# Convolution block by lookup: weight preparation set by the image's rhythm, sums in place, a product split 7 to 2, ranking without negation, an earlier norm and scatter

## The chip, the cores and the metric

One core of a Trainium2 chip runs the kernel. The metric is the device time of one execution in microseconds (us). Before the change three runs took 2664.11, 2668.53 and 2668.79 us; the median is 2668.53. The engines are named as in the profile: PE (TensorE matmuls), PEld (its weight loads), DVE (VectorE), ACT (ScalarE), POOL (GpSimd), SP (the queue that issues most DMAs).

## The reference

Sixteen images of 256 channels and 28 x 28 pixels. The convolutions are replaced by a soft lookup: each channel's 3 x 3 patch is compared with 16 centroids, a softmax of the negated distances gives 16 weights, and these weigh rows of a table.

```python
def amm_conv3x3(x, centroids, w_sub):
    p = patches of x, as (B, pixels, C, 9)
    d = sum(p*p) - 2 * einsum('bncs,cks->bnck', p, centroids) + sum(centroids*centroids)
    attn = softmax(-d, axis=-1)                       # over the 16 centroids
    lut = einsum('cks,cso->cko', centroids, w_sub)
    return einsum('bnck,cko->bno', attn, lut)

def block(h):                                         # h = group norm of x
    out = relu(bn1(amm_conv3x3(h, centroids1, wsub1)))
    out = bn2(amm_conv3x3(out, centroids2, wsub2))
    out = out * sigmoid(relu(mean(out) @ w1 + b1) @ w2 + b2)
    return relu(out + h)

x = x + block(group_norm(x))
```

## The kernel before

**Blocks and steps.** Two layers (`l` = 0, 1) of 16 images (`b`). An image has 256 channels in two halves (`hh`) and 28 rows in two halves (`t`), so four blocks. Work of all engines is put into one list, `at(step, sub, function, ...)`, and issued in the order of (step, sub); each engine, and each DMA queue (SP's and POOL's), then runs its own instructions strictly in that order. A block takes two steps, an image eight; image n of the 32 starts at step 8n. Below, the position of a step is its number modulo eight, and sub orders work inside a step.

**A block.** `patches` loads nine shifted copies of the map from a DRAM copy (`home1`, `home2`) into `pt`, two steps ahead (SP, sub 1.5). `logits` (L386) multiplies by centroids into PSUM (`lg`), ACT takes the exponential (L397). `num_b` (L450) and `num_a` (L436) turn the weights into eight channels' lookup sums and denominators; DVE forms the reciprocal (L478), spreads it (L493) and scales (L512), POOL scales one pair and the ninth tap (L501). Each block ends with nine operands `q` of 128 x 392: four pairs `mm` (taps k = 2mm and 2mm + 1) and a single one (tap 8).

**Products.** The four blocks of an image would need eight products with quarter matrices A11, A12, A21, A22. The kernel uses a Strassen-like form with seven products: sums of the matrices (S1 to S4) and differences of operands, `mix` on POOL (L527, L529). `PRODUCTS` says at which step, relative to 8n, each product runs (sub 2.0) and over which taps; the product of S1 is cut into two parts, at steps 6 and 7. KO is the order of taps, (2, ..., 8, 0, 1); the mixes run in the order of pairs 1, 2, 3, tap 8, pair 0. The five mixes that make S1's operand start at step 5, sub 2.5. Results are put together by `acc_copy`, `acc_add` (L551, L557, L559) and `reg_add` (L564) in `hpads` (one tile of 128 x 900 for each half of the channels); c11, c12, c21, c22 are the quarters (channel half, row half).

**End of an image in layer 0.** `norm_out` (L571, ACT) applies batch norm and ReLU to a quarter, in place. `to_home2` (L592, POOL) then scatters `hpads[o]` to `home2` in DRAM, sorted by a channel ranking, as an indirect DMA in two shifts r = 0 and 1; the four scatters of an image write one tensor, so each waits for the landing of the one before. The next image's `acc_copy` writes the same `hpads`. Image 0 is put aside first (`d_h0`) and scattered later (`h0_load`, `h0_put`), because the ranking comes from its own result: `code_load`, `code_spread` (L612 to L625, DVE, from the centroids of layer 2), `rank_score`, `rank_make` (L652, L653) and so on, in steps 8 to 20.

**Group norm** of the next image runs beside: `gn_stats` (position 0), `gn_mean` (position 1, sub 2.1), `gn_var` (position 3, sub 2.1), each with a small matmul (L324, L338) whose PSUM bank is also used by the `nb` that follows; `gn_apply` and `to_home1` at position 4.

**Preparing the weights of layer 2** during layer 0, because they must be sorted by the ranking: `codes_load` and `codes_put` (centroids), `sub_load` and `sub_put` (the table's weights, 1.15 MB for each half, scattered to `d_wa` and `d_wb`, L680), `prep_wd0` to `prep_wd4` (the centroid matrix: nine small DMAs L717, two products on DVE L726, squares on POOL L285, matmuls L290, sums), `prep_cw0`, `prep_cwa` (L757), `prep_cwb` (L765 to L767), `sums_load`, `sums_put` (S1 to S4 of layer 2, L794). All of them go through one staging buffer `st` of 128 x 1568 (`stage()`), so a new load waits until the last use of the one before is over, and what stands behind it on SP waits too. In layer 2 this buffer serves a numeric safeguard.

Of the kernel before, what the change touches and what calls it, by code (L numbers as in the profile page):

```python
# [17 lines left out]
P = 128  # L18
# [7 lines left out]
K = 16  # L26
# [17 lines left out]
    (5, "A11", 0, KO), (6, "S1", 0, KO[:8]), (7, "S1", 0, KO[8:]), (8, "S3", 1, KO), (9, "S2", 0, KO),  # L44
# [31 lines left out]
def kernel(  # L76
# [530 lines left out]
    def code_spread(o):  # L607
        c2 = idx.pop("c2")
        mean = small.tile([P, S], F32, name="cmean")
        g = c2[:, : S * K].rearrange("p (s k) -> p s k", k=K)  # L610
        d = c2[:, 256 : 256 + S * K].rearrange("p (s k) -> p s k", k=K)
        nc.vector.tensor_reduce(csum[:, o : o + 1], c2[:, : S * K], axis=AX.X, op=ALU.max)  # L612
        nc.vector.tensor_scalar_mul(c2[:, 512 : 512 + S * K], c2[:, : S * K], -1.0)
# [4 lines left out]
        nc.vector.tensor_scalar_mul(mean, mean, 1.0 / K)  # L618
        nc.vector.tensor_sub(d, g, mean.unsqueeze(2).to_broadcast([P, S, K]))
        nc.vector.tensor_scalar_max(c2[:, 256 : 256 + S * K], c2[:, 256 : 256 + S * K], 0.0)  # L620
# [84 lines left out]
    def sub_load(o, part):  # L705
        n = 4 * C if part < 2 else C
        nc.sync.dma_start(stage()[:, :n], wsub2[o * P : (o + 1) * P, part * 4 * C : part * 4 * C + n])

    def sub_put(o, part):
        n = 4 * C if part < 2 else C  # L710
        scatter(d_wa if part < 2 else d_wb, 2 + part, o, pw["st"][:, :n])

    def prep_wd0():
        st = stage()
        nc.gpsimd.memset(st[:, :512], 0.0)
# [21 lines left out]
    def prep_wd4():  # L737
        st = pw.pop("st")
# [3 lines left out]
        nc.sync.dma_start(d_wd[1], st[:, 512:1536])  # L742
# [17 lines left out]
    def prep_cwb(part):  # L760
# [7 lines left out]
        if part == 3:  # L768
            pw.pop("st")
            nc.sync.dma_start(d_cwb, st[:, 512:1536])  # L770

    def sums_load(k0):
        st = stage()
        n = min(2, NS - k0)
        for hh in range(2):
            for o in range(2):
                at0 = 256 * (2 * hh + o)
                if n == 2:
                    nc.sync.dma_start(
                        st[:, at0 : at0 + 256].rearrange("p (s n) -> p s n", n=P),  # L780
                        view(d_wa, (hh * 8 + k0) * P * C + o * P, [[C, P], [P * C, 2], [1, P]]),
                    )
                else:
                    nc.sync.dma_start(st[:, at0 : at0 + P], d_wb[hh * P : hh * P + P, o * P : (o + 1) * P])

    def sums_put(k0):
        st = pw.pop("st")
        n = min(2, NS - k0)
        f = {w: st[:, 256 * i : 256 * i + P * n] for i, w in enumerate(("A11", "A21", "A12", "A22", "S1"))}
        for dst, a, b, op in (  # L790
            ("S1", "A21", "A22", ALU.add), ("A21", "A11", "A21", ALU.subtract),
            ("A22", "S1", "A11", ALU.subtract), ("A12", "A12", "A22", ALU.subtract),
        ):
            nc.gpsimd.tensor_tensor(f[dst], f[a], f[b], op)  # L794
        for n0, w in (("S1", "S1"), ("S3", "A21"), ("S2", "A22"), ("S4", "A12")):
            nc.sync.dma_start(d_ws[n0][:, k0 : k0 + n, :], f[w].rearrange("p (s n) -> p s n", n=P))
# [156 lines left out]
    for l in range(2):  # L953
        for b in range(B):
# [30 lines left out]
            if l == 0:  # L985
                for o in range(2):
# [65 lines left out]
    at(49, 0.6, prep_wd0)  # L1052
    at(50, 0.3, prep_wd1)
    for part in range(3):
        at(51 + 2 * part, 0.02, prep_wd2, part)
        at(51 + 2 * part, 2.1, prep_wd3, part, 51 + 2 * part)
    at(59, 1.9, prep_wd4)
    at(60, 0.6, prep_cw0)
    at(61, 1.9, prep_cwa)
    for part in range(4):  # L1060
        at((67, 68, 75, 76)[part], 2.3, prep_cwb, part)
    at(92, 2.3, load_se)
    for n in range(5):
        at(82 + 8 * n, 0.6, sums_load, 2 * n)
        at(83 + 8 * n, 2.3, sums_put, 2 * n)
# [196 lines left out]
```

## Time and profile before

| what | value |
|---|---|
| median of three runs | 2668.53 us |
| profiled execution | 2669.58 us |
| its span, first to last instruction | 2668.1 us |
| granted clock of PE, mean | 0.994 |
| HBM read, written | 288.93 MB, 79.80 MB |
| `e<-lg` L397 on ACT, 960 times | 821 ns each |
| `qp<-qp,qp` L529 on POOL, 512 times | 1868 ns each |
| `home<-hpad,col` L592 on POOL, 60 times | 1006 ns each; POOL idle before them 180.7 us |

The profiled execution is a separate run, 1.05 us above the median. A line of the timeline reads: start, duration, engine, line of the kernel, operation, what is written and read, shape, count, and in brackets how long the engine stood idle before it and what ended that. PE is busy nearly all the time in every fortieth of the span but the first. PE's granted clock is below 1 only in short stretches: it was 0.50 over 53.8 to 60.6, 122.1 to 125.5, 255.2 to 262.0, 432.7 to 436.1 and at the very end.

PE's own waits between 40 us and the first `nb` of image 14 at 1192.95 us, the longest of them:

| PE waits before | for | us in total, times, longest |
|---|---|---|
| acc L520 | POOL qp L529 | 6.7, 13, 1.5 |
| lg L386 | DVE qp L512 | 6.7, 4, 2.6 |
| nb L450 | DVE gn_dv L330 | 3.7, 1, 3.7 |
| lg L386 | DVE half_sum L557 | 2.1, 1, 2.1 |
| sqp L290 | ACT e L397 | 0.9, 1, 0.9 |
| lg L386 | DMA pt<-home | 0.7, 1, 0.7 |

### The profile page before, as it was taken

The numbers are of one execution on the slowest core, as the hardware profiler recorded it, in microseconds if no ns is written. First come the engines' busy times: TensorE is split into PE (matmuls) and PEld (weight loads), VectorE is DVE, ScalarE is ACT, GpSimd is POOL, SyncE is SP. The second block draws the span as 40 slices with busy tenths as digits, with TensorE's granted clock in tenths as the row PEclk, the third lists the DMA queues.
The fourth block names the chain that finished last, engine by engine and source line by source line (L and its number), as shares of the span: only waits on it lengthen the run. The fifth ranks groups of instructions, "written<-read, shape, count | busy, mean of one in ns | idle before, by whom it ended". The sixth has DMA issues, their size and how long they took to land.

```text
span 2668.1 us, 85705 instructions
## 1 busy us (share of the span) xinstructions
PE 2602.3 (98%) x36984; PEld 1261.0 (47%) x36984; DVE 1773.3 (66%) x3784; ACT 1356.5 (51%) x1874; POOL 1901.2 (71%) x1334
## 2 busy tenths in 40 slices
PE   5899999999999999999999999999999999999997
PEld 2444444444444454444444444444444444444444
DVE  4785666667666656566567767667767667767675
ACT  3344444444444544444455555555555555555653
POOL 3755677656776666776577777788777788787786
PEclk9999999999999999999999999999999999999999
DMA  8556557655567666565574555454445454555451
GB/s 197 156 150 176 157 140 204 185 158 139 142 167 180 175 157 161 147 175 155 136 190 110 114 120 122 117 123 107 118 119 127 113 122 105 120 124 126 114 116 50
DMA packets 219241, 374.39 MB, mean 140 GB/s; under 512 B 30360, under 2 KB 189128, under 8 KB 218856
## 3 DMA queue, kind: packets, MB, share of 16 engines
q1 hardware_dynamic: 211912, 334.87, 51.3%
q0 software_dynamic: 6944, 33.95, 3.6%
q8 instruction: 295, 4.83, 0.8%
q14 instruction: 90, 0.74, 0.1%
HBM read 288.93 MB, written 79.80 MB: 138 GB/s over the span
## 4 chain that ended last, share of the span: by engine, by line
PE 83%; POOL 3%; DMA 3%; issue 1%; ACT 1%; DVE 1%; POOLq 0%; DVEq 0%; ACTq 0%
PE acc L520 44%; PE lg L386 15%; PE na L436 12%; PE nb L450 12%; DMA home<-hpad,col 3%; POOL qp L529 2%; POOL qo L527 0%; POOL home L592 0%; ACT e L397 0%; PE sep L816 0%; PE sep L805 0%; DVE qp L512 0%; DVE rb L493 0%; ACT hpad L571 0%; ACT qo L470 0%
## 5 line engine op out<-in xcount | busy, mean ns | idle before, releaser
L397 ACT ACTIVATE e<-lg 128x784 f32<-128x784 f32 x960 | 738.2, 821 | 704.2 <-PE lg L386 699.6
L529 POOL TENSOR_TENSOR qp<-qp,qp 128x784 f32<-128x784 f32 x512 | 944.2, 1868 | 166.1 <-DVE qp L512 165.6
L520 PE MATMUL acc<-qp,w_S 128*128 128x392 f32 x2048 | 743.3, 503 | 7.8 <-POOL qp L529 6.9
L493 DVE STREAM_SHUFFLE rb<-r 128x392 f32<-128x392 f32 x1024 | 550.2, 603 | 0.0
L520 PE MATMUL acc<-qp,w_A 128*128 128x392 f32 x1536 | 546.6, 499 | 0.0
L520 PEld LDWEIGHTS acc<-qp,w_S 128*128 128x128 f32 x2048 | 376.3, 191 | 356.6 <-POOL qp L529 38.3
L386 PE MATMUL lg<-pt,wd 32*32 32x392 f32 x16384 | 495.7, 505 | 25.8 <-DMA pt<-home 8.1
L520 PEld LDWEIGHTS acc<-qp,w_A 128*128 128x128 f32 x1536 | 284.5, 190 | 247.0 <-DVE qp L512 40.0
L512 DVE TENSOR_TENSOR qp<-na,rb 128x784 f32<-128x784 f32 x352 | 333.3, 971 | 91.6 <-PE na L436 80.7
L464 DVE SCALAR_TENSOR_TENSOR r<-nb,kst,r 128x392 f32<-128x392 f32 x128 | 79.9, 624 | 462.3 <-ACT r L460 448.7
L450 PE MATMUL nb<-e,cwb 64*32 64x392 f32 x8192 | 378.2, 499 | 4.5 <-DVE gn_dv L330 3.7
L436 PE MATMUL na<-e,cwa 64*32 64x392 f32 x8192 | 374.4, 492 | 0.9 <-ACT e L397 0.7
L478 DVE RECIPROCAL r<-r 128x392 f32<-128x392 f32 x128 | 333.2, 2603 | 4.4
L501 POOL TENSOR_TENSOR qp<-qp,rb 128x784 f32<-128x784 f32 x160 | 296.9, 1866 | 2.4
L501 POOL TENSOR_TENSOR qo<-qo,rb 128x392 f32<-128x392 f32 x128 | 131.3, 1026 | 200.1 <-DVE rb L489 200.0
L450 PEld LDWEIGHTS nb<-e,cwb 64*32 64x32 f32 x8192 | 181.5, 108 | 194.3 <-issue 50.9
L386 PEld LDWEIGHTS lg<-pt,wd 32*32 32x32 f32 x16384 | 126.7, 103 | 306.2 <-issue 251.3
L436 PEld LDWEIGHTS na<-e,cwa 64*32 64x32 f32 x8192 | 182.4, 106 | 183.9 <-issue 74.0
L592 POOL DMA_INDIRECT home<-hpad,col x60 | 60.4, 1006 | 180.7 <-DMA home<-hpad,col 78.6
L460 ACT ACTIVATE r<-nb,kst 128x392 f32<-128x392 f32 x128 | 86.7, 678 | 180.2 <-PE nb L450 180.1
L421 POOL TENSOR_TENSOR z<-z,mx 128x1568 f32<-128x1568 f32 x32 | 92.0, 2875 | 86.3 <-DVE mx L415 86.3
L506 ACT COPY qp<-na 128x784 f32<-128x784 f32 x160 | 130.0, 812 | 24.3 <-PE na L436 22.8
(153 smaller groups left out, 1742.7 us busy)
## 6 DMA issues: line engine op xcount, KB each, us to landing
pt<-home SPq DMA_DIRECT2D x768, 209.0 KB
pt<-home SPq DMA_DIRECT2D x756, 104.5 KB
home<-xpad SPq DMA_DIRECT2D x31, 899.0 KB
xt<-in_x SPq DMA_DIRECT2D x30, 784.0 KB
out_dram<-y SPq DMA_DIRECT2D x32, 392.0 KB
w_S<-d_wS SPq DMA_DIRECT2D x4, 576.0 KB
st<-in_wsub SPq DMA_DIRECT2D x4, 512.0 KB
st<-d_wa SPq DMA_DIRECT2D x16, 128.0 KB
```

Of the source, the lines that this page charges most:

```text
L386: nc.tensor.matmul(bk[32 * c : 32 * c + 32, :N].rearrange("p (r w) -> p r w", w=W), lhsT=wts["wd", u["hh"]][32 * i : 32 * i + 32, mm, c, : ...
L397: nc.scalar.activation(eg[:, 2 * i : 2 * i + 2, :], bk[:, :, :N], AF.Exp, scale=2.0)
L421: nc.gpsimd.tensor_tensor(zk, zk, mx.unsqueeze(2).to_broadcast([P, N // 4, K]), ALU.subtract)
L436: nc.tensor.matmul(bs[32 * i : 32 * i + 32, r, :N], lhsT=wts["cwa", u["hh"]][64 * r : 64 * r + 64, mm, i, :], rhs=es[64 * r : 64 * r + 64, ...
L450: nc.tensor.matmul(bs[32 * i : 32 * i + 32, r, :N], lhsT=wts["cwb", u["hh"]][64 * r : 64 * r + 64, mm, i, :], rhs=es[64 * r : 64 * r + 64, ...
L478: nc.vector.reciprocal(u["r"], u["r"])
L493: nc.vector.stream_shuffle(rb[:, r, :], u["r"], mask_of(2 * mm + r))
L501: nc.gpsimd.tensor_tensor(q, q, u.pop(("rb", mm)), ALU.mult)
L506: nc.scalar.copy(pair(u, mm), u.pop(("na", mm))[:, :, :N])
L512: nc.vector.tensor_mul(pair(u, mm), u.pop(("na", mm))[:, :, :N], rb)
L520: nc.tensor.matmul(accs[key][:, :N], lhsT=wl[w][:, k, :], rhs=us["q", k], start=first and n == 0, stop=last and n == len(ks) - 1,)
L529: nc.gpsimd.tensor_tensor(pair(out_u, mm), pair(in0, mm), pair(in1, mm), ALU.subtract)
```

## The change

Five things. The product of S1 is cut 7 to 2 instead of 8 to 1. `code_spread` no longer negates the codes to find the largest magnitude: it takes the minimum and combines it. In layer 0, `norm_out` of c11 moves from sub 1.9 to 0.95 of step 8n + 12, the first scatter of `hpads[0]` from 1.95 to 0.96 (the second stays, at 1.97). The weight sums are formed in place, three taps at a time (three rounds instead of five), with load, sums and store in three different steps. And all of the preparation gets new steps and subs: loads at sub 2.6, behind the patches of the step, and POOL's work mostly at odd positions; `sub_load` brings two parts for each half instead of three, and clearing and storing become functions of their own.

```diff
 PRODUCTS = (
-    (5, "A11", 0, KO), (6, "S1", 0, KO[:8]), (7, "S1", 0, KO[8:]), (8, "S3", 1, KO), (9, "S2", 0, KO),
+    (5, "A11", 0, KO), (6, "S1", 0, KO[:7]), (7, "S1", 0, KO[7:]), (8, "S3", 1, KO), (9, "S2", 0, KO),
...
         nc.vector.tensor_reduce(csum[:, o : o + 1], c2[:, : S * K], axis=AX.X, op=ALU.max)
-        nc.vector.tensor_scalar_mul(c2[:, 512 : 512 + S * K], c2[:, : S * K], -1.0)
         m2 = small.tile([P, 1], F32, name="cm2")
-        nc.vector.tensor_reduce(m2, c2[:, 512 : 512 + S * K], axis=AX.X, op=ALU.max)
-        nc.vector.tensor_scalar_max(csum[:, o : o + 1], csum[:, o : o + 1], m2[:, 0:1])
+        nc.vector.tensor_reduce(m2, c2[:, : S * K], axis=AX.X, op=ALU.min)
+        cs = csum[:, o : o + 1]
+        nc.vector.scalar_tensor_tensor(cs, m2, -1.0, cs, op0=ALU.mult, op1=ALU.max)
...
     def sub_load(o, part):
-        n = 4 * C if part < 2 else C
+        n = (4 + part) * C
         nc.sync.dma_start(stage()[:, :n], wsub2[o * P : (o + 1) * P, part * 4 * C : part * 4 * C + n])
     def sub_put(o, part):
-        n = 4 * C if part < 2 else C
-        scatter(d_wa if part < 2 else d_wb, 2 + part, o, pw["st"][:, :n])
+        scatter(d_wa, 2 + part, o, pw["st"][:, : 4 * C])
+        if part == 1:
+            scatter(d_wb, 4, o, pw["st"][:, 4 * C : 5 * C])
+    def prep_clear():
+        nc.gpsimd.memset(stage()[:, :512], 0.0)
...
+    def prep_keep(dst):
+        nc.sync.dma_start(dst, pw.pop("st")[:, 512:1536])
...
     def sums_load(k0):
-        n = min(2, NS - k0)
+        n = min(3, NS - 1 - k0)
+        for w, t in sums_of().items():
+            hh, o = {"A11": (0, 0), "A21": (0, 1), "A12": (1, 0), "A22": (1, 1)}[w]
+            nc.sync.dma_start(
+                t[:, : n * P].rearrange("p (s n) -> p s n", n=P),
+                view(d_wa, (hh * 8 + k0) * P * C + o * P, [[C, P], [P * C, n], [1, P]]),
+            )
+            if n < 3:
+                nc.sync.dma_start(t[:, n * P :], d_wb[hh * P : hh * P + P, o * P : (o + 1) * P])
+    def sums_make():
+        f = sums_of()
+            ("A22", "A21", "A22", ALU.add), ("A21", "A11", "A21", ALU.subtract),
+            ("A11", "A22", "A11", ALU.subtract), ("A12", "A12", "A11", ALU.subtract),
+            nc.gpsimd.tensor_tensor(f[dst], f[a], f[b], op)
+    def sums_put(k0):
+        for n0, w in (("S1", "A22"), ("S3", "A21"), ("S2", "A11"), ("S4", "A12")):
+            nc.sync.dma_start(d_ws[n0][:, k0 : k0 + 3, :], f[w].rearrange("p (s n) -> p s n", n=P))
...
-                at(g + 12, 1.9, norm_out, l, b, *c11)
+                at(g + 12, 1.9 if l else 0.95, norm_out, l, b, *c11)
...
-                            at(g + 12 + o + (o and r), (1.95, 1.96)[r] if o == 0 else (1.805, 2.9)[r], to_home2, b, o, r)
+                            at(g + 12 + o + (o and r), (0.96, 1.97)[r] if o == 0 else (1.805, 2.9)[r], to_home2, b, o, r)
...
-        at(20 + 3 * o, 0.6, h0_load, o)
+        at(24 + 2 * o, 0.6 + 2 * o, h0_load, o)
         for r in range(2):
-            at(*(((21, 1.77), (22, 2.95)), ((24, 2.95), (25, 1.78)))[o][r], h0_put, o, r)
-        at(32 + 2 * o, 0.6, codes_load, o)
+            at(25 + 2 * o + r, 0.2 if r else 1.9, h0_put, o, r)
+        at(32 + 2 * o, 2.6, codes_load, o)
         for i in range(2):
-            at(33 + 2 * o, 1.78 if o == i == 0 else 1.805, codes_put, o, i)
-        for part in range(3):
-            c = 36 + 6 * o + 2 * part
-            at(c, 0.6, sub_load, o, part)
-            at(c + 1, (1.77, 2.7, 1.78, 1.805)[(3 * o + part) % 4 if o == 0 else (3, 0, 1)[part]], sub_put, o, part)
-    at(49, 0.6, prep_wd0)
-    at(50, 0.3, prep_wd1)
+            at(33 + 2 * o, 1.9, codes_put, o, i)
+        for part in range(2):
+            c = 40 + 8 * o + 2 * part
+            at(c, 2.6, sub_load, o, part)
+            at(c + 1, 1.9, sub_put, o, part)
+    at(56, 1.95, prep_clear)
+    at(57, 1.6, prep_wd0)
+    at(60, 0.3, prep_wd1)
     for part in range(3):
-        at(51 + 2 * part, 0.02, prep_wd2, part)
-        at(51 + 2 * part, 2.1, prep_wd3, part, 51 + 2 * part)
-    at(59, 1.9, prep_wd4)
-    at(60, 0.6, prep_cw0)
-    at(61, 1.9, prep_cwa)
+        c = (65, 67, 73)[part]
+        at(c, 0.02, prep_wd2, part)
+        at(c, 2.1, prep_wd3, part, c)
+    at(75, 1.9, prep_wd4)
+    at(75, 2.7, prep_keep, d_wd[1])
+    at(80, 2.6, prep_cw0)
+    at(82, 1.9, prep_cwa)
     for part in range(4):
-        at((67, 68, 75, 76)[part], 2.3, prep_cwb, part)
+        at((83, 84, 91, 92)[part], (2.3, 1.5, 2.3, 1.5)[part], prep_cwb, part)
+    at(92, 2.7, prep_keep, d_cwb)
     at(92, 2.3, load_se)
-    for n in range(5):
-        at(82 + 8 * n, 0.6, sums_load, 2 * n)
-        at(83 + 8 * n, 2.3, sums_put, 2 * n)
+    for n in range(3):
+        at(96 + 8 * n, 2.6, sums_load, 3 * n)
+        at(97 + 8 * n, 1.9, sums_make)
+        at(98 + 8 * n, 2.6, sums_put, 3 * n)
```

More of the change, by code (lines that the diff above doesn't have):

```diff
@@ L705, in sub_load @@
     def sub_load(o, part):
-        n = 4 * C if part < 2 else C
+        n = (4 + part) * C
         nc.sync.dma_start(stage()[:, :n], wsub2[o * P : (o + 1) * P, part * 4 * C : part * 4 * C + n])
     def sub_put(o, part):
-        n = 4 * C if part < 2 else C
-        scatter(d_wa if part < 2 else d_wb, 2 + part, o, pw["st"][:, :n])
+        scatter(d_wa, 2 + part, o, pw["st"][:, : 4 * C])
[3 more added lines that the diff above has]
+        nc.gpsimd.memset(stage()[:, :512], 0.0)
     def prep_wd0():
-        st = stage()
-        nc.gpsimd.memset(st[:, :512], 0.0)
+        st = pw["st"]
         for s in range(S):
@@ L737, in prep_wd4 @@
     def prep_wd4():
-        st = pw.pop("st")
+        st = pw["st"]
         center_mean(st[:, 512:1536], 1024, nc.gpsimd)
@@ L741, in prep_wd4 @@
         nc.gpsimd.tensor_sub(f, f, kbias.unsqueeze(1).to_broadcast([P, 32, 32]))
-        nc.sync.dma_start(d_wd[1], st[:, 512:1536])
+    def prep_keep(dst):
+        nc.sync.dma_start(dst, pw.pop("st")[:, 512:1536])
     def prep_cw0():
@@ L767, in prep_cwb, with sums_of @@
             nc.gpsimd.tensor_add(f[:, m], f[:, m], ones_b[:, m % 4, :].unsqueeze(1).to_broadcast([P, 4, 32]))
-        if part == 3:
-            pw.pop("st")
-            nc.sync.dma_start(d_cwb, st[:, 512:1536])
+    def sums_of():
+        return {w: pw["st"][:, 3 * P * i : 3 * P * i + 3 * P] for i, w in enumerate(("A11", "A21", "A12", "A22"))}
     def sums_load(k0):
-        st = stage()
-        n = min(2, NS - k0)
[L775 to L789, printed above, removed]
+        stage()
+        n = min(3, NS - 1 - k0)
[7 more added lines that the diff above has]
+                nc.sync.dma_start(t[:, n * P :], d_wb[hh * P : hh * P + P, o * P : (o + 1) * P])
```

6 lines of the change are left out of this document (2 added, 4 removed).

## The prediction

> **What bounds the kernel now.** I read the page first, then the same stretch image by image, then timelines where an image is long.
>
> ```profile
> span 2668.1 us, 85705 instructions
> PE 2602.3 (98%) x36984; PEld 1261.0 (47%) x36984; DVE 1773.3 (66%) x3784; ACT 1356.5 (51%) x1874; POOL 1901.2 (71%) x1334
> PE 83%; POOL 3%; DMA 3%; issue 1%; ACT 1%; DVE 1%; POOLq 0%; DVEq 0%; ACTq 0%
> ```
>
> TensorE is the bound. The change takes no matmul away, so it can only win where TensorE stands still or is clocked down; the chain's shares of POOL and DMA (3% each) say that there is something. The next view cuts the trace at the first `nb` matmul (L450) of an image; columns are length, busy time of each engine, granted clock, DMA share, GB/s. The rows are images 1, 2, 4, 5, 6, 9, 13 and 14 of the first layer.
>
> ```profile
> 122.27:206.35 84.08, 81.83 (x1154) 39.12 (x1154) 62.88 (x144) 36.58 (x50) 50.80 (x38) 0.98 0.54 141
> 206.35:292.38 86.03, 84.05 (x1166) 41.39 (x1155) 51.70 (x124) 37.68 (x52) 58.48 (x58) 0.96 0.63 170
> 373.07:456.78 83.71, 81.63 (x1167) 39.47 (x1155) 51.08 (x120) 38.00 (x52) 56.73 (x43) 0.98 0.66 180
> 456.78:539.55 82.77, 81.00 (x1166) 39.00 (x1155) 50.99 (x120) 37.90 (x52) 55.21 (x42) 1.00 0.62 168
> 539.55:624.42 84.87, 82.74 (x1170) 39.93 (x1160) 55.14 (x125) 38.12 (x52) 54.41 (x41) 1.00 0.61 158
> 786.43:867.27 80.84, 80.40 (x1166) 39.15 (x1155) 50.99 (x120) 38.00 (x52) 56.16 (x50) 1.00 0.64 162
> 1111.01:1192.95 81.94, 81.16 (x1165) 39.16 (x1154) 50.97 (x120) 37.95 (x52) 54.73 (x42) 1.00 0.62 164
> 1192.95:1273.00 80.05, 80.05 (x1164) 38.77 (x1153) 48.73 (x111) 37.99 (x52) 53.59 (x43) 1.00 0.58 149
> ```
>
> Image 14 has PE busy for all of its 80.05 us, and so have the images after it (80.42 us in layer 2). I take it as the ruler. Images 1 to 13 together are 30 us longer than 13 times 80.05, and the stall of 3.7 us before image 1 comes on top: some 34 us is all there is to win. Laying each run of matmuls of an image beside the same run of image 14 shows where each lags; these lags are the terms below. (0.12 us that images 1 to 13 all show at their end is not counted. A position is a step modulo eight.)
>
> **A: ranking without negation.** Before image 1, `nb` waits 3.71 us for DVE's group-norm work, which is queued behind the code ranking:
>
> ```profile
> 113.51 6.33 DVE L613 TENSOR_SCALAR c<-c 128x144 f32<-128x144 f32 x1
> 120.67 0.17 DVE L618 TENSOR_SCALAR cmean<-cmean 128x9 f32<-128x9 f32 x1
> 121.22 0.23 DVE L620 TENSOR_SCALAR c<-c 128x144 f32<-128x144 f32 x1
> ```
>
> ```profile
> 114.32 2.65 POOL L211 TENSOR_TENSOR w_S<-w_A,w_S 128x1152 f32<-128x1152 f32 x1
> 117.87 1.87 POOL L501 TENSOR_TENSOR qp<-qp,rb 128x784 f32<-128x784 f32 x1
> ```
>
> The negation (L613) takes 0.22 us in the other half at 140.37, but 6.33 us here: it ends at 119.84, 0.1 us after POOL's unbroken run of 112.51 to 119.74. Taking it out removes the stall only if the instructions behind it do not stand in the same place: L618 (9 columns) and L620 (144) are of the same kind, and at 141.41 L618 took 0.91 us, until a POOL instruction ended. Most such waits in this trace end at the next POOL boundary (L653 twice 1.93 to 1.95 us, L726 1.03 and 2.07); this one missed three. If L618 and L620 get in at 116.96 and 117.94, DVE is at the group norm by about 119, the 3.7 us wait shrinks below 1 and the half clock that follows it (0.50 over 122.1 to 125.5, 1.58 us of lag) goes: 4.3 to 5.3 us. If they too wait to 119.74, only the removed L613 and its neighbour's order are saved, 0.5 us. I take 3.0, between both, nearer the end that most rows show. The new two-operand maximum replaces L616 (0.21 us) and costs the same.
>
> The Trainium skill, SBUF — State Buffer, section "Who interferes with whom", says that a Vector instruction with two SBUF inputs also contends with a GpSimd instruction that reads SBUF. The trace agrees in one place: beside DVE's sum L211 at 94.79 (1.42 us) a POOL L529 took 2.99 us, its mean being 1.87. By that rule the new maximum may stand where the negation stood; A would be 0.5.
>
> **B: norm and scatter a stage sooner, product split 7 to 2.** At the end of an image POOL scatters `hpads` in four pieces, each waiting for the one before to land:
>
> ```profile
> 734.09 1.09 POOL L592 DMA_INDIRECT home<-hpad,col  x1 [3.14 <-ACT hpad L571]
> 740.67 0.97 POOL L592 DMA_INDIRECT home<-hpad,col  x1 [5.49 <-DMA home<-hpad,col]
> 748.23 1.03 POOL L592 DMA_INDIRECT home<-hpad,col  x1 [1.24 <-PE acc L520]
> 749.29 5.49 POOL L529 TENSOR_TENSOR qp<-qp,qp 128x784 f32<-128x784 f32 x3
> 755.71 1.85 POOL L529 TENSOR_TENSOR qp<-qp,qp 128x784 f32<-128x784 f32 x1
> ```
>
> ```profile
> 757.61 0.93 PE L520 MATMUL acc<-qp,w_S 128*128 128x392 f32 x2 [0.39 <-POOL qp L529]
> ```
>
> The five differences for S1 start behind the third piece, the last of them (pair 0, taps 0 and 1) ends at 757.56, and S1's last tap of that step waits. In the worst image, 2, the second piece landed so late that ACT's copy into `hpads` stood, and all of ACT with it:
>
> ```profile
> 252.31 0.49 ACT L551 COPY hpad<-acc 128x392 f32<-128x392 f32 x1 [8.26 <-DMA home<-hpad,col]
> ```
>
> With the norm at 0.95, ACT can do it after the two exponentials that end at 728.86, as c11's sum is done on DVE about 1 us earlier: 0.72 us, so the first piece is issued near 730 instead of 734.1, the second near 736.5 instead of 740.7. The third is then bound by POOL's scaling, not by a landing; the differences start 1 to 3 us sooner. By the split, pair 0 is needed only in the next step, some 5 us later. One tap (0.66 us on PE) moves from one step to the next, so PE's sum is the same; in layer 2, where PE never idles, it costs nothing. Queued behind the earlier pieces on POOL is only the scaling of the next step, which waits for DVE anyway (1.6 us at 904.36). Lags that go: image 2 5.86, image 3 0.53, image 5 2.60, images 8 to 13 0.62, 0.67, 1.08, 1.00, 1.18, 1.38. Sum 14.9, at least 12 if image 2 keeps half.
>
> **C: preparation moved.** Image 4 loses 3.53: SP's load of weights stands until the scatter of 413.23 lands at 420.82, the patches behind it go out 1.4 us late, logits wait 2.08 and run at half clock after it (0.50 over 432.7 to 436.1). The new loads sit at 2.6, behind the patches. Image 6 loses 0.77 and 0.44 to nine patch-delaying DMAs (0.57 us each) of prep_wd0 and to its two DVE products, 3.0 us long against POOL; they move to 1.6 and to position 4, where POOL is nearly idle. Image 7's 1.06 and image 13's 0.39 are late transfers and side work. Sum 6.2, at least 3.
>
> What the new places cost: prep_cwa now stands in position 2 ahead of the scaled copies. In image 10 DVE is free there at 876.69, POOL busy until 877.87, and the first L512 starts at 879.12. Four products of 0.34 (the shortest L757) from 877.87 end at 879.2, then the sum and two shuffles of 1.6 us: L512 is 1.8 late, the second logits, at 880.83, have 0.75 slack after its end at 880.08, so 1.1 is lost; 0 to 3 by the long L757 of 1.96. The three squares' matmuls all fall on group-norm steps as one did before; that one cost 1.27, the others 0.65 and 1.50, so 0.1 more. The sums become 12 POOL instructions of about 0.84 (L285, same 384 columns) in 3.48 us of idle POOL before the image, and 12 stores for 20 and 16 loads for 20; one instruction too long at most delays differences with 4.9 us of slack. h0's second scatters wait on POOL for a landing (2.9 to 7.6 us by L680) ahead of differences with that slack; SP's waits at 2.6 stand where it would wait for logits. Unbooked collisions: I put 1.0, 0 to 9. Rank_make's 2.26 in image 1 stays.
>
> **Sum.** 3.0 + 14.9 + 6.2 - 1.1 - 0.1 - 1.0 = 21.9. The profiled execution took 2669.58 (span 2668.1 and 1.5 around it), 1.05 above the median of 2668.53. 2669.58 - 21.9 = 2647.7; on the scale of the median 2646.6. I say 2647.
>
> **Rivals.**
> 1. The port wait passes on: the new maximum, L618 or L620 ends at 119.8. For it: L613 itself, three missed boundaries. Against: all other rows. A is 0.5, 2.5 less: 2649.1. Chance 0.24. The two-input rule above leads here.
> 2. Collisions in the new places: three of the preparation scatters (steps 28, 43, 75) hold POOL just ahead of the first piece of `hpads`, and three images lose what images 4 or 5 lost (2.6 to 3.5): 9 more, 2656. For it: each scatter blocks 1 us and lands in up to 7.6. Against: the split. Chance 0.12.
> 3. Little changes: differences still start late, as DVE's shuffles, not the scatters, release POOL, and the moved stalls come back elsewhere one for one; A alone is left, 2666. Against: image 14 with its third piece at 1234.93 lost nothing. Chance 0.08.
> 4. Slower: the first piece now runs beside the patches of its step (issued 2 us after it), they land late, and logits wait as in image 4, 2.08 and 1.42 at half clock, in all 15 scattering images: 52 - 22 = 30 more, 2699. It decides once patches land after the step's first logits; so far they were late at 549.46 (0.70) and in image 4 after 1.4 us of delay. Against: before, the piece ran beside the same patches' tails and the stores to home1. Chance 0.06.
>
> **How the numbers follow.** My forecast has 0.50; its own range is 2643 to 2652. With rivals 1 and 2 it makes 0.86; 2641 (A at 5.3, nothing lost in the new places, 1 us of spread between runs) to 2658 holds 0.8 of it all. About 0.2% (5.3 us) is what a measurement of this kernel can tell from no change: faster 0.86, same 0.08, slower 0.06.
>
> **What would show it.** Right: images 2 to 13 at 80.1 to 81, only those with square matmuls (7 and 8) and cwa (10) above; no PE wait on POOL L529 at S1; first piece about 24 us after an image's first `nb` instead of 28.4; clock at 1.00 from 135 on; DVE's reduction behind L612 short and the 3.7 us wait under 1. Wrong: a DVE TENSOR_SCALAR ending at 119.8 (rival 1), POOL's L592 with long waits behind a preparation scatter (2), logits waiting for `pt` (4).

## The result, and the profile after

The changed kernel takes 2652.59 us (median of 4 runs, 2650.44 to 2653.86) where before took 2668.66 beside it (4 runs): the ratio is 0.9942, with a 95% interval of 0.9925 to 0.9959. It is faster, by 16.1 us; the forecast was 21.9 less. The profiled execution took 2652.68, against 2669.58 before, so the traces account for 16.9.

The page of the profile has the same three lines to compare:

```profile
span 2651.2 us, 85709 instructions
PE 2594.3 (98%) x36984; PEld 1265.2 (48%) x36984; DVE 1771.8 (67%) x3782; ACT 1356.7 (51%) x1874; POOL 1901.3 (72%) x1326
PE 96%; DVE 2%; DMA 1%; issue 0%; POOL 0%; SPq 0%; ACT 0%; another core or an unknown queue 0%; DVEq 0%; POOLq 0%
```

In the chain of waits (last line) TensorE went from 83% to 96%, POOL from 3% to 0%, DMA from 3% to 1%: POOL's part of the chain is gone. DVE, which was at 1%, is at 2%.

The same cut by image, at the first `nb` matmul; rows are images 2, 4, 8, 9 and 14 (length, busy time of PE, PEld, DVE, ACT, POOL, clock, DMA share, GB/s):

```profile
203.16:285.00 81.84, 81.79 (x1164) 39.86 (x1154) 51.78 (x124) 37.99 (x52) 56.67 (x55) 1.00 0.61 160
366.31:446.93 80.62, 80.58 (x1166) 39.98 (x1155) 50.95 (x120) 37.89 (x52) 54.72 (x41) 1.00 0.63 169
690.37:773.20 82.83, 82.06 (x1170) 40.06 (x1159) 52.09 (x122) 38.02 (x52) 53.07 (x40) 1.00 0.55 149
773.20:853.23 80.03, 80.03 (x1166) 39.38 (x1155) 54.71 (x122) 38.12 (x52) 56.24 (x40) 1.00 0.63 162
1176.41:1256.99 80.58, 80.53 (x1164) 39.01 (x1152) 48.70 (x111) 37.89 (x52) 52.93 (x41) 1.00 0.56 153
```

The long images 2, 4, 5 and 6 lost 4.2, 3.1, 2.2 and 3.8 us, and the granted clock, which before was 0.50 for 6.8 and 3.4 us in images 2 and 4, stays at 1.00 from image 2 until 2639 us. But among images 2 to 13 only image 9 reaches 80.03. Most others stop at 80.3 to 81.6, with PE "busy" almost throughout: the gaps in them are at most 0.4 us, and their pieces are longer. Image 8 is 2.0 longer than before's 80.78, and the old ruler, image 14, 0.5.

Images 2 to 16 together went from 1226.49 to 1214.05 us: 12.4 less. I use this sum below, because everything before image 2 moves on its own: the first `nb` of image 2 came at 206.35 before and at 203.16 after, but in the nine kernels below that leave code_spread at its steps it came anywhere between 196.7 and 204.8, with stretches of 3.4 or 6.8 us at half clock in varying places. The sums over images 2 to 16 of the changed kernel and of the three that differ from it only before image 2 lie between 1213.77 and 1214.99. The remaining 1.3 us of the 16.9 lie in layer 2.

Two places show what went wrong. The first is the stall ahead of image 1. It is still there; DVE and POOL around it, and TensorE's wait:

```profile
110.51 7.26 DVE L616 SCALAR_TENSOR_TENSOR csum<-cm,csum 128x1 f32<-128x1 f32 x1
117.69 0.29 DVE L617 TENSOR_REDUCE cmean<-c 128x9 f32<-128x144 f32 x1
```

```profile
110.58 1.83 POOL L529 TENSOR_TENSOR qp<-qp,qp 128x784 f32<-128x784 f32 x1
112.37 2.61 POOL L211 TENSOR_TENSOR w_S<-w_A,w_S 128x1152 f32<-128x1152 f32 x1
...
115.92 1.84 POOL L501 TENSOR_TENSOR qp<-qp,rb 128x784 f32<-128x784 f32 x1
```

```profile
119.62 1.84 PE L450 MATMUL nb<-e,cwb 64*32 64x392 f32 x24 [4.39 <-DVE gn_dv L330]
```

The new maximum (L616, one column) stands for 7.26 us, ends at 117.77 where POOL's unbroken run ends (117.76), and `nb` waits 4.39 us instead of 3.71. In most of the kernels below that have the same code at the same place, the wait is divided in another way; part A of the experiments shows it.

The second is the second logits at position 4 of image 4:

```profile
390.48 1.07 POOL L592 DMA_INDIRECT home<-hpad,col  x1 [1.44 <-ACT hpad L571]
390.78 0.23 PEld L386 LDWEIGHTS lg<-pt,wd 32*32 32x32 f32 x31 [0.64 <-issue]
390.78 1.46 PE L386 MATMUL lg<-pt,wd 32*32 32x392 f32 x32
391.73 0.10 PEld L386 LDWEIGHTS lg<-pt,wd 32*32 32x32 f32 x1 [0.72 <-issue]
391.74 0.68 ACT L460 ACTIVATE r<-nb,kst 128x392 f32<-128x392 f32 x1 [1.55 <-PE lg L386]
```

The piece takes 1.46 us where it takes 0.94 elsewhere. Thirty-one of its 32 weight loads go out at once; the last one waits for nothing that the profile shows and starts at 391.73. ACT's split_r (L460, which reads `nb`) starts at the same moment, 0.9 us after `nb` was done. Both are 0.18 us behind the end of POOL's issuing of the early scatter. I call this a hold. The same shows in images 3 (twice) to 8 and 12 to 15, 0.23 to 0.79 us each time, 5.6 in sum, and under the two gathers of rank_look in image 2, 1.8. It does not show in image 1, which scatters nothing, nor in images 9 to 11, where POOL was busy with the preparation and the scatter started 0.4 to 1.1 us behind the start of the logits, nor under the early scatters of images 2 and 16, 0.2 and 0.8 us behind it.

### The profile page after: what moved, and what is told of

It reads as the page before. It is cut to its first block, busy times and chain, and to the rows that moved or that the text cites. A ratio compares the mean times of both kernels' runs of the same rounds, so it can differ in the third digit from the quotient of the medians.

```text
span 2651.2 us, 85709 instructions
## 1 busy us (share of the span) xinstructions
PE 2594.3 (98%) x36984; PEld 1265.2 (48%) x36984; DVE 1771.8 (67%) x3782; ACT 1356.7 (51%) x1874; POOL 1901.3 (72%) x1326
## 4 chain that ended last, share of the span: by engine, by line
PE 96%; DVE 2%; DMA 1%; issue 0%; POOL 0%; SPq 0%; ACT 0%; another core or an unknown queue 0%; DVEq 0%; POOLq 0%
PE acc L520 51%; PE lg L386 17%; PE nb L450 14%; PE na L436 13%; DMA pt<-home 1%; DVE rb L493 1%; DVE qp L512 0%; PE sqp L290 0%; DVE csum L616 0%; PE sep L821 0%; DVE r L478 0%; DVE gn_st L318 0%; POOL qp L529 0%; PE sep L810 0%; DMA xt<-in_x 0%
## 5 line engine op out<-in xcount | busy, mean ns | idle before, releaser
L529 POOL TENSOR_TENSOR qp<-qp,qp 128x784 f32<-128x784 f32 x512 | 943.5, 1867 | 166.2 <-DVE qp L512 165.7
L520 PE MATMUL acc<-qp,w_S 128*128 128x392 f32 x2048 | 732.7, 500 | 0.9 <-DVE qp L512 0.7
L450 PEld LDWEIGHTS nb<-e,cwb 64*32 64x32 f32 x8192 | 190.8, 107 | 184.1 <-issue 29.1
L460 ACT ACTIVATE r<-nb,kst 128x392 f32<-128x392 f32 x128 | 86.7, 677 | 174.7 <-PE nb L450 163.9
L527 POOL TENSOR_TENSOR qo<-qo,qo 128x392 f32<-128x392 f32 x128 | 131.1, 1024 | 0.0
```

Source lines behind the costliest of these rows:

```text
L450: nc.tensor.matmul(bs[32 * i : 32 * i + 32, r, :N], lhsT=wts["cwb", u["hh"]][64 * r : 64 * r + 64, mm, i, :], rhs=es[64 * r : 64 * r + 64, ...
L520: nc.tensor.matmul(accs[key][:, :N], lhsT=wl[w][:, k, :], rhs=us["q", k], start=first and n == 0, stop=last and n == len(ks) - 1,)
L527: nc.gpsimd.tensor_tensor(out_u["q", 8], in0["q", 8], in1["q", 8], ALU.subtract)
L529: nc.gpsimd.tensor_tensor(pair(out_u, mm), pair(in0, mm), pair(in1, mm), ALU.subtract)
```

## The experiments

Each is the changed kernel with one edit, unless said otherwise. The ratio is to the kernel before on the same chip.

| kernel | median us | ratio, 95% interval | images 2 to 16, us |
|---|---|---|---|
| the change | 2652.59 | 0.9942 (0.9925 to 0.9959) | 1214.05 |
| e2_negate | 2652.19 | 0.9934 (0.9917 to 0.9950) | 1214.94 |
| e9_pointer | 2652.65 | 0.9941 (0.9921 to 0.9961) | 1213.77 |
| e1_codes_later | 2648.51 | 0.9923 (0.9906 to 0.9939) | 1214.99 |
| e4_norm_late | 2659.38 | 0.9959 (0.9943 to 0.9976) | 1220.16 |
| e3_eight_one | 2657.00 | 0.9966 (0.9955 to 0.9977) | 1217.32 |
| e7_prep_old | 2649.25 | 0.9944 (0.9922 to 0.9966) | 1217.07 |
| e6_squares | 2648.96 | 0.9942 (0.9924 to 0.9961) | 1211.49 |
| e5_scatter_after | 2650.07 | 0.9926 (0.9910 to 0.9943) | 1215.60 |
| e8_look | 2652.09 | 0.9950 (0.9934 to 0.9966) | 1215.22 |
| e10_pause | 2647.25 | 0.9923 (0.9901 to 0.9946) | 1211.85 |
| e11_all | 2641.00 | 0.9902 (0.9872 to 0.9932) | 1209.48 |
| e12_no_pause | 2636.93 | 0.9908 (0.9892 to 0.9924) | 1204.37 |

**The code ranking (part A).** First the negation put back:

```diff
+nc.vector.tensor_scalar_mul(c2[:, 512 : 512 + S * K], c2[:, : S * K], -1.0)
...
-nc.vector.tensor_reduce(m2, c2[:, : S * K], axis=AX.X, op=ALU.min)
-cs = csum[:, o : o + 1]
-nc.vector.scalar_tensor_tensor(cs, m2, -1.0, cs, op0=ALU.mult, op1=ALU.max)
+nc.vector.tensor_reduce(m2, c2[:, 512 : 512 + S * K], axis=AX.X, op=ALU.max)
+nc.vector.tensor_scalar_max(csum[:, o : o + 1], csum[:, o : o + 1], m2[:, 0:1])
```

> The changed kernel with the old code_spread, negation and all. Theory (the wait goes on to the next instruction that must share with POOL): the negation waits for the same POOL run as L616 does, the gap before nb is 3.7 instead of 4.4 us, and the time is 0 to 0.7 us below the changed kernel's, 2651.9 to 2652.6: too little to measure by times, to be read in the profile. Rival (the forecast's step): taking the negation out did save 3.0 us, and this kernel takes 2655.6.

Measured: 2652.19, a gap of 4.95 us ahead of `nb` (not 3.7, so even the sign of that small difference was not as expected). The 3.0 us of the forecast are not there: in the times (2652.19 against 2652.59) the negation's removal is worth nothing that can be seen.

Then the maximum in another form, one tensor and a 128x1 scalar:

```diff
-nc.vector.scalar_tensor_tensor(cs, m2, -1.0, cs, op0=ALU.mult, op1=ALU.max)
+nc.vector.tensor_scalar(cs, m2, -1.0, cs, op0=ALU.mult, op1=ALU.max)
```

> The changed kernel with L616 as a tensor_scalar that takes csum as its 128x1 scalar, so that it reads one tensor instead of two. Theory: the form of L616 decides only which instruction waits; the next ones of code_spread (the tensor_scalar on 128x9, the two-tensor subtract on 128x144) meet the same unbroken POOL run, so one of them takes the wait, ends within 0.3 us of POOL's run, the gap ahead of nb stays above 1.5 us and the time at 2651 to 2653. Rival: only L616's two tensors wait; with one it takes 0.2 us, code_spread ends by 113, the gap goes and the time is that of the run with the code work moved, some 2648.5.

```profile
111.26 0.21 DVE L616 TENSOR_SCALAR csum<-cm,csum 128x1 f32<-128x1 f32 x1
...
111.72 7.13 DVE L618 TENSOR_SCALAR cmean<-cmean 128x9 f32<-128x9 f32 x1
```

In DVE's timeline L616 now takes 0.21 us, and L618, nine columns and one tensor, takes the wait, 7.13 us, to the end of POOL's run at 118.83. The gap is 4.19 us. The wait passes from one instruction to the next that needs what POOL holds.

How long the group stands differs from kernel to kernel, though. The changed code_spread stands at the same steps in seven more kernels below. In e10_pause L616 (L620 in its numbering) takes 7.63 us, and the gap is 4.60. In the other six (e3 to e8) it takes 0.20 to 1.61 us, and those behind it wait in turn, each to the end of the POOL instruction that is running. e3_eight_one:

```profile
111.20 1.57 DVE L618 TENSOR_SCALAR cmean<-cmean 128x9 f32<-128x9 f32 x1
112.80 2.69 DVE L619 TENSOR_TENSOR c<-c,cmean 128x144 f32<-128x144 f32 x1
115.52 0.93 DVE L620 TENSOR_SCALAR c<-c 128x144 f32<-128x144 f32 x1
```

There the gaps ahead of `nb` are 1.80, 3.21, 1.91, 2.28, 1.91 and 1.91 us. So the group can get in at each end of a POOL instruction and still come late. What decides between the two courses is not shown, and with one trace of each kernel neither is the part of the gap that the removed negation saves.

Last, the work moved away from that run. Both halves of the codes share one tile; loads at step 8:

```diff
-    for o in range(2):
-        at(8 + 2 * o, 0.6, code_load, o)
-        at(9 + 2 * o, 1.9, code_spread, o)
+    at(8, 0.6, code_load)
+    at(11, 1.9, code_spread, 0)
+    at(12, 0.97, code_spread, 1)
```

> The changed kernel with both halves' code work (loads in one tile, code_spread) moved to steps 11 and 12, where POOL has pauses. Theory: the 128x1 scalar_tensor_tensor of L616 (7.26 us, ending with POOL's unbroken run) held back the norm's DVE instructions behind it, and so made the 4.39 us TensorE gap at 115.23 and the half clock at 120.09 to 123.50. Then both go: 4.4 + 1.6 = 6.0 us less than the changed kernel's 2652.6, some 2646.6 (2645 to 2649), and the clock is 1.00 from about 59 us on. Rival: something else of step 9 (the statistics themselves, POOL's products) is as late, the gap stays above 3 us and the time at 2651 to 2653.

The windows of images 0 and 1, and TensorE's timeline at the old stall:

```profile
39.99:116.03 76.04, 66.74 (x1113) 29.06 (x1103) 53.50 (x127) 35.34 (x48) 45.34 (x33) 0.94 0.75 189
116.03:197.88 81.85, 80.14 (x1165) 39.38 (x1154) 64.89 (x150) 38.06 (x52) 53.13 (x40) 1.00 0.57 145
```

```profile
116.03 0.94 PE L450 MATMUL nb<-e,cwb 64*32 64x392 f32 x16
```

`nb` follows the logits without a gap; image 0 lasts 76.04 us instead of 80.35, image 1 81.85 instead of 83.54, the latter at clock 1.00. The median is 4.1 lower; the 6.0 of the two images are within the play of the start (e7_prep_old, with the code work in its old place, has 76.67 and 81.85). The cause of the stall is shown: it is where code_spread stands, not what it computes. The two later kernels with the same move (e11, e12) have no gap either, and the eleven traces without it have 1.8 to 4.95 us.

**Early scatter and split (part B).** The norm of c11 and its first scatter put back, with the split kept:

```diff
-at(g + 12, 1.9 if l else 0.95, norm_out, l, b, *c11)
+at(g + 12, 1.9, norm_out, l, b, *c11)
-at(g + 12 + o + (o and r), (0.96, 1.97)[r] if o == 0 else ...
+at(g + 12 + o + (o and r), (1.95, 1.96)[r] if o == 0 else ...
```

> The changed kernel with the norm of c11 and its first scatter back at 1.9 and 1.95 of step g+12; the 7 to 2 split stays. Three theories. (a) The early scatter alone cleared the waits for POOL's mixes, 14.9 us in the trace of before, and it costs about 5.1 us at the second logits: this kernel takes 2652.6 + 14.9 - 5.1 = 2662. (b) The split alone does it: no PE wait on POOL L529, no longer logits pieces, 2652.6 - 5.1 = 2647.5. (c) Each takes part of the waits: between the two, 2650 to 2658, with waits for L529 in image 2 and 5 alone.

TensorE's waits for POOL in image 2 (total, times, longest):

```profile
PE acc L520 <- POOL qp L529: 1.2, 3, 0.7
```

Theory (c) is the nearest, though 2659.38 lies above its 2658: images 2 and 9, where POOL also prepares, take 84.8 and 81.9 us, 2.9 and 1.9 more than with the early scatter; image 16 takes 1.3 more. The waits for POOL are only 1.2 us in image 2 and 0.2 in image 9. Much of the rest are pieces held as above under other scatters, 1.2, 1.0 and 1.1 us in these three images. Images 8 and 10 to 13 stay without a wait. The other half, the split alone undone:

```diff
-(6, "S1", 0, KO[:7]), (7, "S1", 0, KO[7:])
+(6, "S1", 0, KO[:8]), (7, "S1", 0, KO[8:])
```

> The changed kernel with the products of S1 split 8 to 1 again; norm and scatter stay early. Theory, after the run with the late norm lost 7 us with waits for POOL's mixes in images 2 and 9 alone: early scatter and split each suffice in images 8 and 10 to 13, so this kernel has no wait or short ones for POOL L529 and takes 2652 to 2654. Rival: the split is what keeps the last mix off the path; TensorE waits for L529 by 0.4 to 1.0 us in each of images 8 to 13 and more in 2 and 5, 2657 to 2662.

Measured: no wait for L529 from image 1 on, 3.3 us more in images 2 to 16, spread over them with 0.76 in image 3 as the largest; the time of 2657.0 is above the theory's 2654, and I found no line for all of the difference. So, with the new preparation in place, either step leaves images 8 and 10 to 13 without a wait, and images 2 and 9 need the early scatter; the two gains are not added to one another. No run has the new preparation without both steps, and in some images it may clear the waits by itself: in e4_norm_late the third piece of the scatter goes out 41.5 us behind the first `nb` of images 12 and 13, where it was 43.2 and 43.3 before, and image 14 of before, with 41.98, had no wait.

**Preparation (part C).** The kernel of before with the new code_spread, the split and the early scatter, but the old preparation:

> The kernel of before with the new code_spread, the 7 to 2 split and the early norm and scatter, but with the old timetable and the old pieces of the weight preparation. It shows what moving the preparation is worth. Forecast's step: moving gained 6.2 us and cost 1.1 + 0.1 + 1.0, so this kernel takes 2652.6 + 4.0 = 2656.6. Rival 1: with the mixes off the path the old preparation is hidden as well: 2652 to 2653. Rival 2: the squares' three steps cost the changed kernel 3.6 us where the old ones cost 1.9 and cwa 0.7, and the gains are 3.5 (image 4), 1.2 and 1.1 (images 6 and 7): 2654 to 2655.

Two windows, images 2 and 8:

```profile
196.72:283.63 86.91, 84.68 (x1167) 41.27 (x1155) 51.80 (x124) 38.00 (x52) 59.54 (x58) 0.98 0.63 173
692.56:772.59 80.03, 80.03 (x1166) 39.39 (x1155) 50.97 (x120) 38.11 (x52) 56.36 (x50) 1.00 0.58 155
```

Images 2 to 6 are 9.3 us longer than with the new preparation, images 7 to 13 6.2 shorter: 3.0 in favour of the new one, where 4.0 were expected. Over half of the 9.3 is image 2, 86.9 against 81.85 us. There the early scatter does its work, as ACT's copy no longer waits for a landing, but logits wait 2.2 us for patches, the clock is 0.50 from 271.4 to 274.8, and two `na` pieces take 3.9 and 4.6 us instead of 2.92. Image 4, at 81.51, is only 0.9 longer than with the new preparation. The times (2649.25 and 2652.59, ratios 0.9944 and 0.9942) do not tell the two apart. The 6.2 have two parts: the squares fall in earlier images, and in images 7 to 13 some old piece of POOL work happens to keep the early scatter back until 0.4 to 1.5 us behind the start of the logits. There those pieces last 0.94 us, and images 8 to 12 80.03.

The three squares in steps without group-norm statistics:

```diff
-        c = (65, 67, 73)[part]
+        c = (61, 63, 69)[part]
```

> The changed kernel with the three squares of the layer-1 weights (center_sq, center_add) at steps 61, 63, 69 instead of 65, 67, 73. In the changed kernel each stands in a step that also has a group-norm statistic: gap 0.41, 0.34, 0.41 us ahead of sqp on the norm's DVE instruction that reads the same PSUM bank. Theory: the gaps go at 61 and 69, which have no statistic, and 63 has none either: 1.2 us less, 2651.4, the sqp matmuls themselves (0.88, 0.88, 0.67 us) stay. Rival: the squares' loads are not in time that early (landed after step 60) and TensorE or DVE waits for the loads by a microsecond or more: 2653 to 2656.

The gaps of 0.41, 0.34 and 0.41 us are down to one of 0.28. Images 7 and 8 together take 163.3 instead of 164.7 us, 1.4 less where 1.2 was expected. The 2.6 in the sum include 1.0 of image 13 and 0.7 of image 3 that have no link to the edit, and the ratio, 0.9942, is that of the change.

**The held logits.** The norm and the scatter behind split_r:

```diff
-at(g + 12, 1.9 if l else 0.95, norm_out, l, b, *c11)
+at(g + 12, 1.9 if l else 1.055, norm_out, l, b, *c11)
-(0.96, 1.97)[r] if o == 0 else ...
+(1.056, 1.97)[r] if o == 0 else ...
```

> The changed kernel with the norm of c11 behind split_r (1.055 of step g+12 instead of 0.95) and the first scatter behind it, so that POOL's 1.07 us of issuing comes after the second logits instead of 0.3 us ahead of them. Theory: while POOL issues that scatter, the last weight load of the logits and ACT's split_r are held until about 0.2 us after its end; moved, all logits pieces there take 0.94 us, and the sum of 0.49, 0.79, 0.54, 0.51, 0.23, 0.53, 0.50, 0.54, 0.53, 0.53, 0.40 = 5.6 us is saved: 2647.0 (2646 to 2649). Rival 1: the stall belongs to the TensorE's own instruction stream at that place, and stays: 2652 to 2653. Rival 2: the later scatter makes patches or mixes late, and a wait of a microsecond per image comes in its place: 2655 to 2665.

```profile
396.38 0.97 POOL L592 DMA_INDIRECT home<-hpad,col  x1 [4.39 <-DMA home<-hpad,col]
...
397.08 3.43 PE L436 MATMUL na<-e,cwa 64*32 64x392 f32 x64
```

All the second logits but image 3's take 0.94 us, but nothing is saved (1215.60). The second scatter waits for the first to land (4.39 us), so it came later too, and now its issuing lies over `na`: 3.43 us instead of 2.92, with a weight load that resumes at 397.66, 0.3 us behind the scatter. Neither rival in its own form: the hold went with the scatter, and cost the same one piece further on.

The two gathers of rank_look, which in the changed kernel's image 2 lie over a logits piece of 2.64 us:

```diff
-        at(18, 2.1, rank_sum, o)
-        at(18, 2.15, rank_look, o)
+        at(18, 1.9, rank_sum, o)
+        at(18, 1.95, rank_look, o)
```

> The changed kernel with rank_sum and rank_look of step 18 at 1.9 and 1.95 instead of 2.1 and 2.15, so that POOL's two gathers (1.11 and 0.97 us, at 215.53 and 216.95) end before the logits at 216.72. Theory: POOL's issuing of an indirect DMA holds TensorE's weight loads when small tiles run under it; that made the logits piece at 216.72 take 2.64 us instead of 0.94. Moved by about a microsecond, the piece takes 0.94 to 1.2 and image 2's period falls by 1.2 to 1.8 us: 2651.1. Rival: the piece is long for another reason (the DVE instruction L512 ahead of the bank, the code there) and stays at 2.6 us: 2652.6, or more because DVE's work of step 19 comes later.

```profile
212.50 5.00 PE L436 MATMUL na<-e,cwa 64*32 64x392 f32 x64
212.58 1.11 POOL L667 DMA_INDIRECT idx<-in_ids,ri  x1 [0.17 <-issue]
...
217.44 0.94 PE L386 MATMUL lg<-pt,wd 32*32 32x392 f32 x32
```

The logits are at 0.94 us, and the `na` that now lies under the gathers takes 5.00 instead of 2.92. Nothing is won (82.11 us in image 2), but a second kind of transfer, on other data, holds another product. Third, the scatter alone held back, by an instruction of POOL that multiplies ten rows by 1.0:

```diff
+    def pause(b):
+        r = region(0, b, 0, 0)[:, :10]
+        nc.gpsimd.tensor_mul(r, r, one.unsqueeze(2).to_broadcast([P, 10, W]))
...
+                if b:
+                    at(g + 12, 0.955, pause, b)
```

> The changed kernel with a POOL instruction of no effect ahead of each first scatter (it multiplies 10 rows of the half map by 1.0), which holds the scatter back by some 0.6 to 1.0 us. Norm and all orders stay. Theory: the scatter's issuing starts 0.4 us or later behind the start of the second logits, as in images 9 to 11 of the changed kernel, the pieces there take 0.94 us, and its second scatter still ends ahead of the next logits: images 4 to 8 and 12 to 15 fall by 0.2 to 0.5 us each, about 4.5 us in all, 2648.1. Rival 1: the stall moves to the next tiled piece as it did with the norm moved: sum unchanged, 2652. Rival 2: POOL's extra work delays the mixes: above 2653.

Images 4 and 5 (and 12) reach 80.02, images 10 and 14 get 0.6 longer, and the sum falls by 2.2, not 4.5; the median by 5.3, more than expected, with overlapping intervals. ACT is still held there: its exponentials start 0.83 us behind the logits, 0.26 behind the scatter's end, and cost nothing in that place.

**Together.** The moved code work, the pause and the squares:

> The changed kernel with three edits that the runs pointed to: the code work at steps 11 and 12, the pause ahead of the first scatter, the squares at steps 61, 63, 69. Theory: they act in different images and add up: 4.1 (measured) + 4.5 (expected) + 2.6 (sum over images 2 to 16 of the squares' run) = 11.2 less than 2652.6, 2641.4 (2639 to 2645). Rival: the pause does nothing, 2646.

2641.00, near the 2641.4 that were added up, 0.9902 (0.9872 to 0.9932). But the parts are not those of the sum: images 2 to 16 are 4.6 us shorter than in the change, where the pause and the squares were booked with 7.1, and image 2 starts 6.3 earlier, where the code work was booked with 4.1. That the total fits is luck in part. And the same without the pause:

> The kernel with all three edits less the pause: code work at steps 11 and 12, squares at 61, 63, 69. It shows by times, not by the profile alone, what the pause is worth. Theory (scatter issuing under small tiles costs TensorE about half a microsecond an image): 4.5 more than the 2641.0 with the pause, 2645.5 (2644 to 2648), and the sum over images 2 to 16 near the 1211.5 of the squares' run. Rival: the stall is small outside the profiled execution, and the time is within 1.5 of 2641.0.

This last run was made on another chip than the eleven before it; before itself took 2661.74 there, 4 to 7 us less than beside the others. By ratio, 0.9908 (0.9892 to 0.9924) against 0.9902, the two kernels can't be told apart, as the rival said. And the trace of this run speaks against my theory in its simple form. The place of image 4 shown above, and the window of image 2:

```profile
379.66 1.07 POOL L592 DMA_INDIRECT home<-hpad,col  x1 [1.42 <-ACT hpad L571]
379.95 0.23 PEld L386 LDWEIGHTS lg<-pt,wd 32*32 32x32 f32 x32 [0.64 <-issue]
379.95 0.94 PE L386 MATMUL lg<-pt,wd 32*32 32x392 f32 x32
380.08 0.68 ACT L460 ACTIVATE r<-nb,kst 128x392 f32<-128x392 f32 x1 [0.71 <-PE nb L450]
```

```profile
195.51:275.54 80.03, 80.03 (x1166) 39.37 (x1155) 51.68 (x124) 38.02 (x52) 56.72 (x55) 1.00 0.64 164
```

The scatter starts 0.3 us ahead of the logits and takes 1.07 us, as in the changed kernel, and nothing is held: 32 weight loads at once, the piece takes 0.94 us, ACT starts 0.06 behind `nb`. Images 2 to 5 take 80.02 or 80.03. Not one piece is long under an indirect DMA in this trace, the gathers of image 2 included. So there was no hold for a pause to take away, and what the pause is worth where there are holds is not shown. The eleven other experiments have such a hold in every trace.

The trace of before shows no hold either, although some of its gathers and scatters lay under logits in the same way. The second gather of rank_look, first before, then in the changed kernel:

```profile
219.92 0.94 PE L386 MATMUL lg<-pt,wd 32*32 32x392 f32 x32
220.16 0.97 POOL L667 DMA_INDIRECT idx<-in_ids,ri  x1 [0.31 <-DVE qp L512]
```

```profile
216.72 2.64 PE L386 MATMUL lg<-pt,wd 32*32 32x392 f32 x32
216.95 0.97 POOL L667 DMA_INDIRECT idx<-in_ids,ri  x1 [0.31 <-DVE qp L512]
```

The gather starts 0.24 and 0.23 us behind the logits, and only the second piece is long. Scatters that start 0.27 us ahead of logits (414.91 and 1307.72 before) left them at 0.94 us as well. So the overlap is needed for the hold, but it isn't enough. Whether the rest of it is the chip, or how a program came to lie in memory, stays open, as no kernel has a trace from two chips and the chip of the traces of before and of the change is not known.

## Why the prediction was right, and where not

The direction and the range (2641 to 2658) held, and in most images so did the mechanism of the largest term, B; the time was 5.6 us above the 2647. That the sum came this near is luck in part: A gave less than was said, and gains were booked under B and C that needed both.

- **Part A failed**, at the step "I take 3.0, between both, nearer the end that most rows show". Rival 1 came true: the wait passes on. Its price, 0.5, agrees with e2_negate, whose time shows no gain, and e9_pointer shows that a third instruction would have taken the wait in the new one's place. The mark was named as a TENSOR_SCALAR ending with POOL's run; it was the new maximum. But the step was wrong in a second way. The forecast had the wait shrink below 1 if L618 and L620 get in at the ends of POOL's instructions. In e3 to e8 they do, and the wait is 1.8 to 3.2 us, because L619 between them waits as well (2.69 us in e3); it was not counted. The Trainium skill's rule (SBUF — State Buffer, "Who interferes with whom") is that a DVE instruction with two SBUF inputs contends with a GpSimd instruction that reads SBUF. L616, 7.26 us on a single column, and L619 agree with it. The same section of the Trainium skill names tensor_scalar as a kind that can contend, as L618 did for 7.13, and tensor_reduce as one that never does on this chip, as L612, L614 and L617 with 0.3 us. I had the rule and gave it too little weight against rows of other instructions. The start was 3.2 us shorter all the same, which is within the play of the first 125 us.
- **Part B's mechanism was right in most images**: the first piece goes out 24.0 to 24.2 us behind the image's first `nb` in eight images and at most 26.4 (24 was said) instead of 28.4, and no image of the first layer has a TensorE wait for POOL L529. That early scatter, split and perhaps the new preparation do the same work in most images (e3, e4) was not seen. The largest entry, image 2 with 5.86, does not belong to B alone: with B and the old preparation the image takes 86.9 us (e7), with the new preparation and the late scatter 84.8 (e4), with both 81.85, where it took 86.03 before. Rival 3, little changes, and rival 4, patches that come late, did not happen.
- **Part C** was near by luck: 4.0 net was forecast, 3.0 shown by the sum of images (e7). But image 2 alone, booked under B, gives 5.1, and image 4, booked here with 3.5, gives 0.9, as without the new preparation it is already down from 83.7 to 81.5. Its squares were booked at 0.1 more; e6 shows 1.4 in images 7 and 8. cwa's 1.1 is 0.7 in image 10.
- **The collisions were mis-sized**: "I put 1.0, 0 to 9". The one that mattered in this trace was not on the list of rivals: not a scatter that waits, but a transfer under whose issuing TensorE and ACT stand, 5.6 us under the scatters and 1.8 under the gathers. As the trace of before has the same overlaps without a hold, it could not be read there, and it is not shown that the change brought the holds. B and C less their costs were 18.9 us; images 2 to 16 gave 12.4. With the holds (7.4) and the squares (1.4) added back it would be 21.2, some 2 more than forecast; this is an estimate from the lengths of the pieces. The run without holds points the same way: its images 2 to 16 take 1204.37, 22.1 less than before. It has the moved squares too, and its trace may come from another chip than that of before, so it supports the reading without proving it.

## What to carry to other kernels

When a DVE instruction stands for microseconds beside POOL, changing or removing it helps only if the next instruction of its group doesn't need the same thing, and every member of the group has to be counted; moving the whole group to where POOL pauses took the stall away. When an indirect DMA is moved, look also at what runs during the microsecond in which POOL issues it, and at the next transfer that waits for its landing. Steps that remove the same wait are priced together, once.

## What the hardware showed that I had not expected

- A waiting DVE instruction does not always get in at the next end of a POOL instruction: L616 stood past four ends (110.61, 112.41, 114.98, 115.95) until POOL paused. It stood so in two of the eight traces with this code at this place; in the other six each wait ended at the next end of a POOL instruction. The same section of the Trainium skill says, of DVE's 2-port modes, that whoever issues first gets the shared pair of ports for the whole instruction. The six traces fit that; in the two the wait went through a whole run of instructions.
- In eleven of twelve experiments' traces, and in that of the change, TensorE's weight loads in pieces of small tiles, and ACT, stood still until 0.2 to 0.5 us behind the end of a scatter's instruction on POOL, with no wait recorded. Under the two gathers the loads came in bursts (6 of 32 between two stops in the changed kernel). The same section of the Trainium skill says: "PE and ACT never wait on anyone." That speaks of SBUF ports; these rows show a hold of another kind, and the twelfth trace and that of before show that it need not come. What holds them is not shown.
